# Norm's root put on Y at its eviction, one sum as final update; the second quartic's transposes read without steps; seven sets; the first image without trips

## The chip, the cores and the metric

The kernel runs on one core of a Trainium2 chip. The metric is the device time of one execution in microseconds, the median of several runs. The core has five engines that work through their own instruction lists and wait for each other by semaphores: TensorE (PE, matrix products, with PEld for its weight loads), VectorE (DVE), ScalarE (ACT), GpSimd (POOL) and SyncE (SP), which here only issues transfers. Products land in PSUM, 8 banks of 128x512 floats; DVE and ACT move them from there to SBUF (an eviction).

## The reference

The input is 32 images of 32 channels of 128x128 floats. Two residual layers follow each other; both start with a group norm over pairs of channels (16 groups).

```python
def _L0_conv_ref(A):                       # for each of 1024 matrices
    normA = jnp.sqrt(jnp.sum(A2 * A2, axis=(1, 2)))
    Y = A2 / normA[:, None, None]
    Z = I
    for _ in range(5):
        T = 0.5 * (3.0 * I - jnp.matmul(Z, Y))
        Y = jnp.matmul(Y, T)
        Z = jnp.matmul(T, Z)
    return Y * jnp.sqrt(normA)[:, None, None]
...
x = x + _L0_conv_ref(_gn(x))
x = x + _L1_conv_ref(_gn(x), L1_conv_weights1, L1_conv_weights2)
```

The first layer is five steps of a coupled Newton iteration for a matrix square root, for each of the 1024 matrices. The second is a spectral convolution: a Fourier transform of each image, a 32x32 channel mix on two corners of the spectrum, and the inverse transform.

## The kernel before, in words

**Newton.** The five steps are regrouped into two "quartics" and a last step, so that a matrix needs few products. Four channels form a group, one tile of 128x512; there are 8 groups in an image and 256 in all. `products` makes the four 128x128 products of a group into one PSUM bank, and `transposed` four transposes by TensorE. Each group runs through the generator `newton` (L377), in which every `yield` hands over to the next group. In order it makes: v = plus(mb m) and q = plus(v w) (the first quartic, L347), y from q m, m from q y, mb as the transpose of m, r = mb + eye on GpSimd, then v and q again (the second quartic), then w and y (tile y4) from q m and q y, t = plus(w q), and at last t y, times the root of the norm, added to the input tile xt. `plus` (L269, the sum at L272) evicts on DVE with one scalar_tensor_tensor, `taken` (L261) on ACT.

**Far and near.** The quartic needs w, the transpose of v plus r. For the images below FIRST = 20 ("far") w takes a trip in place of TensorE's time: DVE transposes 32x32 blocks of v into the tile turn (L354), SyncE stores that to a DRAM buffer (L356), loads it back with the blocks in transposed places (L360), and GpSimd adds r (L367). For the other 12 images ("near") TensorE transposes v, and DVE adds r in the eviction. A far group has two trips and 11 sets of four products or transposes, a near group has two sets of transposes more. On the far side the tiles come from the pool `sets` and, in turns, from a second pool `early` (the pair of counts in `rooms`, L249), which is given up when the far groups are done, to make room for the second layer.

**Order.** The main loop (L857) goes round the lanes: LANES = 6 groups are under way at a time, each advances by one `yield` in a round, and a new far group enters every FAR = 17/6 rounds (17 yields in six lanes). Near groups enter every 13/4 rounds, with at most LESS = 4 lanes in use. Beside the lanes, one step of a norm, of the statistics of the next image (`prep`), of the forward transform (`posts`), the spectrum and the inverse (`backs`) is made in a round. The program is recorded in this order; then a planner, which has its own idea of how long instructions take, orders the instructions of each engine. What is wrapped in `kept` keeps its order: the transfers, and the staging. Each engine then works strictly through its list.

**Staging.** `fetch` loads a group twice, as b (from x) and as xt (from the transposed input), and `staged` (L316) applies the norm: b on ACT (L324), and m from xt, two of its four channels on GpSimd (L331) and two on ACT (L324). The four sums at the end of `newton` (L397) multiply by the root of the norm, a value sn for each channel, and add to xt in place. After that `settle` (L405) stores xt, folds it for the forward transform on GpSimd (L412) and takes statistics on DVE (L416).

**Second layer.** When all images of a block of 21, 8 or 3 (GROUPS) have their spectrum, the channel mix (L529, L585) and the inverse transforms (L709 to L783) of that block run between the near groups, or at the end.

The lines that the change touches, and what calls them:

Of the kernel before, what the change touches and what calls it, by code (L numbers as in the profile page):

```python
# [25 lines left out]
ALU = mybir.AluOpType  # L29
# [4 lines left out]
P = 128  # L34
B = 32
C = 32
G = 16
LANES, LESS = 6, 4
FAR, NEAR = 17 / 6, 13 / 4
GROUPS = (21, 8, 3)  # L40


# [5 lines left out]
MS = -QA * QS  # L48
FIRST = GROUPS[0] - 1
# [15 lines left out]
def conv_preact_kernel(  # L65
# [8 lines left out]
    nc = tc.nc  # L74
# [65 lines left out]
    def bank():  # L140
        return ps8.tile([P, 4, P], F32, tag="ps", name="ps")
# [33 lines left out]
    kept = tc.keep_in_program_order  # L175
# [70 lines left out]
        yield  # L246


    rooms = dict(b=(6, 2), xt=(10, 4), x=(4, 2), r=(4, 3), v=(3, 3), w=(3, 3), q=(3, 1), y=(4, 2))  # L249
    rooms.update(m=(3, 2), mb=(2, 1), t=(3, 1), y4=(2, 1), turn=(0, 3))  # L250
    turns = dict.fromkeys(rooms, 0)

    def four(tag, far):
        n, more = rooms[tag]
        if far:
            turns[tag] += 1
            if turns[tag] % (n + more) >= n:
                return early.tile([P, 4, P], F32, tag=tag + "_early", name=tag, bufs=more)
        return sets.tile([P, 4, P], F32, tag=tag, name=tag, bufs=n)

    def taken(ps, tag, far, f=1.0):  # L261
        t = four(tag, far)
        if f == 1.0:
            nc.scalar.copy(t, ps)
        else:
            nc.scalar.mul(t, ps, f)  # L266
        return t

    def plus(ps, f, t, tag, far):  # L269

        s = four(tag, far)
        nc.vector.scalar_tensor_tensor(s, ps, f, t, ALU.mult, ALU.add)  # L272
        return s

    def blocks(t):


        return t.rearrange("p c x -> p (c x)").rearrange("p (a c j) -> p a c j", a=4, c=4)

    def plus_eye(mb, far):  # L280

        r = four("r", far)
        if far:
            nc.gpsimd.tensor_tensor(
                blocks(r).rearrange("p a c j -> p c a j"),
                mb.rearrange("p c (a j) -> p c a j", a=4),
                eye.rearrange("p c (a j) -> p c a j", a=4),
                ALU.add,
            )
        else:  # L290
            nc.gpsimd.tensor_tensor(r, mb, eye, ALU.add)  # L291
        return r

    def products(lhsT, rhs):
        ps = bank()
        for j in range(4):
            nc.tensor.matmul(ps[:, j, :], lhsT[:, j], rhs[:, j], start=True, stop=True)  # L297
        return ps

    def transposed(t):  # L300
        ps = bank()
        for j in range(4):
            nc.tensor.transpose(ps[:, j, :], t[:, j, :], ident)
        return ps

    raw = {}

    def fetch(b, g):
        xt, t = four("xt", b < FIRST), four("b", b < FIRST)
        kept(nc.scalar.dma_start(out=t, in_=x[b, :, 4 * g : 4 * g + 4, :]))  # L310
        kept(nc.scalar.dma_start(out=xt, in_=xt_in[b, :, 4 * g : 4 * g + 4, :]))
        raw[b, g] = xt, t
# [2 lines left out]

    def staged(b, g, nm, sc, offm, sn, scr, off):  # L316

        m = four("x", b < FIRST)
        xt, mb = raw.pop((b, g))

        def on_scalar(t, x, offset, scale, c):
            c = slice(c, c + 1)
            kept(
                nc.scalar.activation(t, x, AF.Identity, bias=offset[:, c], scale=scale[:, c])  # L324
            )

        for j in range(4):
            c = 4 * g + j
            if j < 2:
                kept(  # L330
                    nc.gpsimd.tensor_scalar(  # L331
                        m[:, j, :],
                        xt[:, j, :],
                        nm[:, c // 2 : c // 2 + 1],
                        sc[:, c : c + 1],
                        ALU.add,
                        ALU.mult,
                    )
                )
            else:  # L340
                on_scalar(m[:, j, :], xt[:, j, :], offm, sc, c)
            on_scalar(mb[:, j, :], mb[:, j, :], off, scr, c)
            yield
        ready.append((xt, m, mb, plus_eye(mb, b < FIRST)))
        yield

    def quartic(m, mb, r, far):  # L347


        v = plus(products(mb, m), -1 / (QA * QR * QS), m, "v", far)  # L350
        if far:

            t = four("turn", far)
            nc.vector.transpose(blocks(t), v.rearrange("p c (i b) -> p b c i", b=4))  # L354
            held = dram.tile([P, 512], F32, name="turn", tag="turn", bufs=8)
            kept(nc.sync.dma_start(out=held, in_=t.rearrange("p c x -> p (c x)")))  # L356
            yield
            w = four("w", far)
            kept(
                nc.sync.dma_start(  # L360
                    out=blocks(w).rearrange("p a c j -> p a (c j)"),
                    in_=held.rearrange("(a i) (b x) -> (i b) a x", a=4, b=4),
                )
            )
            yield
            yield
            nc.gpsimd.tensor_tensor(w, w, r, ALU.add)  # L367
            w = blocks(w).rearrange("p a c j -> p c a j")
        else:
            yield  # L370
            w = plus(transposed(v), 1.0, r, "w", far)
        yield
        q = plus(products(v, w), 1 / (16 * QS * QS), eye, "q", far)
        yield
        return q

    def newton(g, sn, xt, m, mb, r, far):  # L377


        q = yield from quartic(m, mb, r, far)  # L380
        y = taken(products(q, m), "y", far, 1 / MS)
        yield
        m = taken(products(q, y), "m", far, MS)
        yield
        mb = taken(transposed(m), "mb", far, QR * QS / MS)
        r = plus_eye(mb, far)
        yield
        q = yield from quartic(m, mb, r, far)
        pw, py = products(q, m), products(q, y)
        w, y = taken(pw, "t", far, 1 / MS), taken(py, "y4", far)  # L390
        yield
        t = plus(products(w, q), -0.5 * EYE / 1.5, eye, "t", far)
        yield
        ps = products(t, y)
        for j in range(4):
            c = 4 * g + j
            nc.vector.scalar_tensor_tensor(  # L397
                xt[:, j, :], ps[:, j, :], sn[:, c : c + 1], xt[:, j, :], ALU.mult, ALU.add
            )
        yield  # L400

    folds = {}
# [389 lines left out]
    def step(queue):  # L792
        if queue and next(queue[0], queue) is queue:
            queue.pop(0)
# [6 lines left out]
    todo = [(b, g) for b in range(B) for g in range(C // 4)]  # L801
    fetches = list(todo)
    stages = list(todo)
    ready = []
# [48 lines left out]
    fetch(*fetches.pop(0))  # L853
    stage()
    fetch(*fetches.pop(0))
    rounds = 0
    while todo or any(lanes) or posts or specs or prods or backs:  # L857
        tail = not todo and not any(lanes)
        if early and len(settled) >= FIRST * (C // 4):
            change()  # L860
        if tail and not posts and not late:

            phase.close()
            late.append(ctx.enter_context(tc.tile_pool(name="late", bufs=1)))
            for kk in range(2, KK):
                late_wts.append(late[0].tile([P, 2, 4, 4, C], F32, name=f"wt{kk}_late"))
                nc.gpsimd.dma_start(out=late_wts[-1], in_=wk[kk])
        for i in range(LANES):
            step(norms)
            far = todo and todo[0][0] < FIRST  # L870
            room = lanes[i] is None and (far or LANES - lanes.count(None) < LESS)
            if todo and room and rounds >= due:
                due = max(due, rounds - 1) + (FAR if far else NEAR)
                while norms:
                    step(norms)
                b, g = todo.pop(0)
                xt = ready[0][0]
                lanes[i] = (b, g, xt, newton(g, made[b][3], *ready.pop(0), far))
                if stages:
                    stage()  # L880
            if lanes[i] is not None:
                b, g, xt, steps = lanes[i]
                if next(steps, lanes) is lanes:
                    lanes[i] = None
                    end(b, g, xt)
            if i == 1:
                step(preps)
            if i == 2 or tail:
                step(specs)
            if i == 3 or tail:  # L890
                step(posts)
            if i == 0 or tail:
                step(prods)
            if i == 0 and (rounds % 5 or len(ended) > B - 6) or tail and not (posts or specs):
                step(backs)
        rounds += 1
# [64 lines left out]
```

## Time and profile before

| | |
|---|---|
| time, median of 3 runs | 3322.49 us (3322.23 to 3326.34) |
| span of the profiled execution | 3310.1 us |
| granted TensorE clock, mean | 0.967 |
| PE, weight loads | 91%, 86% of the span |
| DVE, POOL, ACT | 75%, 58%, 50% |
| POOL sum w (L367), one of 128x512 | 1275 ns, 320 of them |
| ACT eviction, constant factor (L266) | 593 to 598 ns |
| ACT staging of 128x128 (L324) | 482 to 485 ns |
| POOL staging of 128x128 (L331) | 450 ns |

A row of the groups gives the line, engine, operation, tiles written and read with their shape, the count, then busy time and mean length of one, then the idle time of the engine ahead of it with what ended it. Busy time counts overlapping instructions once, so that busy over count is the pace, and the mean is the length of one. A float product of 128x128 is two PE instructions and a transpose is one, so a set of four products is 8 instructions. In the waits a line such as "PE ps <- DVE q" tells how long PE stood still until a DVE instruction that wrote q was done. PE is busiest in every stretch from 100 to 3200 us. The first 100 us are the start, with PE working 55 of them, and the last 110 the tail, where only the last block's inverse is left.

### The profile page before, as it was taken

What the parts mean: (1) busy time and instruction counts of PE and PEld (TensorE: products, weight loads), DVE (VectorE), ACT (ScalarE), POOL (GpSimd) and SP (SyncE); (2) the same over time, 40 slices, a digit from 0 to 9 for tenths busy, and PEclk for the clock granted to TensorE, in tenths of its full rate; (3) what the DMA queues carried; (4) which work ended last, traced back from release to release, by engine and by line L of the source; (5) the groups of instructions that cost most, each with busy time, mean ns of one, the idle gap of its engine ahead of it and who ended that gap; (6) DMA issues with size and microseconds to landing.
All of it is one profiled execution on the core that took longest, in us unless ns stands there. A gap on an engine that the chain in (4) does not pass through costs nothing. (4 is left out here: it accounts for less than half of the span.)

```text
span 3310.1 us, 77971 instructions
## 1 busy us (share of the span) xinstructions
PE 3001.5 (91%) x29376; PEld 2856.1 (86%) x29376; DVE 2477.9 (75%) x6440; ACT 1664.8 (50%) x3588; POOL 1935.0 (58%) x2120
## 2 busy tenths in 40 slices
PE   4999999999999999999999999999899989999854
PEld 4988898998998888899989999888888888898853
DVE  5887888887888887888888676577677767766645
ACT  2555554555555555555555555554455545546533
POOL 3666666666666666667666443255556656635542
PEclk9999999999999999999999999999999999999985
DMA  4656665665666565666665236765656767666577
GB/s 154 210 186 191 185 207 179 198 196 181 197 195 188 185 192 184 198 193 205 188 192 185 94 98 190 226 210 182 211 196 207 251 195 236 208 218 204 182 262 245
DMA packets 485768, 645.85 MB, mean 195 GB/s; under 512 B 91152, under 2 KB 264464, under 8 KB 485392
## 3 DMA queue, kind: packets, MB, share of 16 engines
q1 hardware_dynamic: 369904, 421.66, 39.5%
q10 hardware_dynamic: 113472, 211.86, 20.6%
q0 software_dynamic: 2016, 7.34, 0.6%
q8 instruction: 233, 3.82, 0.5%
q14 instruction: 143, 1.17, 0.1%
HBM read 402.95 MB, written 237.76 MB: 194 GB/s over the span
## 5 line engine op out<-in xcount | busy, mean ns | idle before, releaser
L367 POOL TENSOR_TENSOR w<-w,r 128x512 f32<-128x512 f32 x320 | 407.4, 1275 | 408.7 <-DMA w<-turn 328.9
L297 PE MATMUL ps<-w,v 128*128 128x128 f32 x4096 | 555.5, 279 | 19.3 <-POOL w L367 14.9
L297 PE MATMUL ps<-y,q 128*128 128x128 f32 x4096 | 556.8, 281 | 3.8 <-ACT y L266 3.8
L324 ACT ACTIVATE b<-b,a_off,a_scr 128x128 f32<-128x128 f32 x1024 | 474.0, 485 | 119.8 <-issue 66.6
L297 PEld LDWEIGHTS ps<-w,v 128*128 128x128 f32 x4096 | 505.2, 194 | 28.7 <-POOL w L367 17.2
L297 PEld LDWEIGHTS ps<-y,q 128*128 128x128 f32 x4096 | 513.1, 197 | 6.8 <-ACT y L266 4.9
L412 POOL TENSOR_TENSOR fold<-xt 128x256 f32<-128x256 f32 x512 | 363.8, 730 | 235.0 <-DVE xt L397 209.2
L272 DVE SCALAR_TENSOR_TENSOR q<-ps,eye 128x512 f32<-128x512 f32 x512 | 347.0, 682 | 108.3 <-PE ps L297 106.7
L706 POOL TENSOR_TENSOR yt<-yt,d 128x512 f32<-128x512 f32 x236 | 297.6, 1286 | 161.4 <-ACT d L765 142.2
L297 PE MATMUL ps<-m,q 128*128 128x128 f32 x2048 | 295.2, 289 | 83.3 <-DVE q L272 82.6
L354 DVE STREAM_TRANSPOSE turn<-v 128x512 f32<-128x512 f32 x320 | 357.9, 1119 | 7.0
L297 PEld LDWEIGHTS ps<-m,q 128*128 128x128 f32 x2048 | 259.6, 199 | 101.1 <-DVE q L272 79.0
L291 POOL TENSOR_TENSOR r<-b,eye 128x512 f32<-128x512 f32 x96 | 122.4, 1275 | 346.9 <-issue 294.5
L397 DVE SCALAR_TENSOR_TENSOR xt<-ps,a_t_s,xt 128x128 f32<-128x128 f32 x1024 | 289.6, 340 | 36.9 <-PE ps L297 35.4
L192 DVE BATCH_NORM_STATS2 a_st<-xs 128x6 f32<-128x128 f32 x1024 | 229.2, 278 | 109.1 <-DMA xs<-in_xt 108.8
L266 ACT ACTIVATE t<-ps 128x512 f32<-128x512 f32 x256 | 153.2, 598 | 311.9 <-PE ps L297 288.0
L272 DVE SCALAR_TENSOR_TENSOR v<-ps,x 128x512 f32<-128x512 f32 x256 | 174.9, 683 | 178.9 <-PE ps L297 166.0
L272 DVE SCALAR_TENSOR_TENSOR v<-ps,m 128x512 f32<-128x512 f32 x256 | 175.2, 684 | 174.5 <-PE ps L297 160.1
L297 PE MATMUL ps<-y,t 128*128 128x128 f32 x2048 | 282.7, 282 | 23.5 <-DVE t L272 23.4
L297 PE MATMUL ps<-m,mb 128*128 128x128 f32 x2048 | 279.7, 280 | 18.4 <-ACT mb L266 11.6
L266 ACT ACTIVATE y<-ps 128x512 f32<-128x512 f32 x256 | 152.6, 596 | 276.2 <-PE ps L297 267.4
L297 PE MATMUL ps<-x,b 128*128 128x128 f32 x2048 | 279.1, 280 | 7.3 <-issue 5.6
(124 smaller groups left out, 6052.1 us busy)
## 6 DMA issues: line engine op xcount, KB each, us to landing
turn<-turn SPq DMA_DIRECT2D x320, 256.0 KB
w<-turn SPq DMA_DIRECT2D x320, 256.0 KB
b<-in_x ACTq DMA_DIRECT2D x256, 256.0 KB
xt<-in_xt ACTq DMA_DIRECT2D x256, 256.0 KB
xs<-in_xt ACTq DMA_DIRECT2D x256, 256.0 KB
mid<-xt SPq DMA_DIRECT2D x256, 256.0 KB
yt<-mid SPq DMA_DIRECT2D x128, 512.0 KB
out<-yt SPq DMA_DIRECT2D x108, 512.0 KB
```

The source lines that it names most:

```text
L192: nc.vector.bn_stats(st[:, 4 * i + c, :], tiles[i][:, c, :])
L266: nc.scalar.mul(t, ps, f)
L272: nc.vector.scalar_tensor_tensor(s, ps, f, t, ALU.mult, ALU.add)
L291: nc.gpsimd.tensor_tensor(r, mb, eye, ALU.add)
L297: nc.tensor.matmul(ps[:, j, :], lhsT[:, j], rhs[:, j], start=True, stop=True)
L324: nc.scalar.activation(t, x, AF.Identity, bias=offset[:, c], scale=scale[:, c])
L354: nc.vector.transpose(blocks(t), v.rearrange("p c (i b) -> p b c i", b=4))
L367: nc.gpsimd.tensor_tensor(w, w, r, ALU.add)
L397: nc.vector.scalar_tensor_tensor(xt[:, j, :], ps[:, j, :], sn[:, c : c + 1], xt[:, j, :], ALU.mult, ALU.add)
L412: nc.gpsimd.tensor_tensor(f[:, :, 64 * half : 64 * half + 64], xt[:, :, 0:64], xt[:, :, 64:128], op)
L706: engine.tensor_tensor(yh, yh, d, op)
```

## The change

- **Root on Y.** The factor sn moves from the last sum to the eviction of y4. In place of one copy of 128x512 on ACT there are four scalings of 128x128, each by its channel's sn. The last update becomes one tensor_tensor of 128x512 on DVE in place of four scalar_tensor_tensors of 128x128.
- **Transposes without steps.** In the second quartic of a far group DVE reads v in runs of 32 neighbours instead of every fourth element. The rows that come back must then go elsewhere, which takes four loads of 32 partitions each in place of one of 128. The first quartic stays as it is.
- **Seven sets.** LANES goes from 6 to 7, with buffers added in `rooms`. A far group gets three yields more (one after each q, one after t), so that it lives for 20 rounds, and FAR becomes 20/7.
- **First image without trips.** `is_far` leaves image 0 out, so it goes the near way, with at most four lanes in use. Near images, image 0 among them, now stage all four channels of m on GpSimd.

```diff
-LANES, LESS = 6, 4
-FAR, NEAR = 17 / 6, 13 / 4
+LANES, LESS = 7, 4
+FAR, NEAR = 20 / 7, 13 / 4
...
-    rooms = dict(b=(6, 2), xt=(10, 4), x=(4, 2), r=(4, 3), v=(3, 3), w=(3, 3), q=(3, 1), y=(4, 2))
-    rooms.update(m=(3, 2), mb=(2, 1), t=(3, 1), y4=(2, 1), turn=(0, 3))
+    rooms = dict(b=(6, 2), xt=(10, 5), x=(4, 3), r=(4, 3), v=(3, 3), w=(3, 3), q=(3, 3), y=(4, 3))
+    rooms.update(m=(3, 3), mb=(2, 1), t=(3, 2), y4=(2, 2), turn=(0, 3))
...
+    def is_far(b):
+        return 0 < b < FIRST
...
-            if j < 2:
+            if j < 2 or not is_far(b):
                 kept(
                     nc.gpsimd.tensor_scalar(
...
-    def quartic(m, mb, r, far):
+    def quartic(m, mb, r, far, wide):
...
-            nc.vector.transpose(blocks(t), v.rearrange("p c (i b) -> p b c i", b=4))
+            form = "p c (b i) -> p b c i" if wide else "p c (i b) -> p b c i"
+            nc.vector.transpose(blocks(t), v.rearrange(form, b=4))
...
-            kept(
-                nc.sync.dma_start(
-                    out=blocks(w).rearrange("p a c j -> p a (c j)"),
-                    in_=held.rearrange("(a i) (b x) -> (i b) a x", a=4, b=4),
-                )
-            )
+            wb = blocks(w).rearrange("p a c j -> p a (c j)")
+            if wide:
+                for b in range(4):
+                    rows = slice(32 * b, 32 * b + 32)
+                    src = held[:, P * b : P * b + P].rearrange("(a i) x -> i a x", a=4)
+                    kept(nc.sync.dma_start(out=wb[rows], in_=src))
+            else:
+                src = held.rearrange("(a i) (b x) -> (i b) a x", a=4, b=4)
+                kept(nc.sync.dma_start(out=wb, in_=src))
...
         q = plus(products(v, w), 1 / (16 * QS * QS), eye, "q", far)
         yield
+        if far:
+            yield
         return q
...
-        w, y = taken(pw, "t", far, 1 / MS), taken(py, "y4", far)
-        yield
-        t = plus(products(w, q), -0.5 * EYE / 1.5, eye, "t", far)
-        yield
-        ps = products(t, y)
+        w, y = taken(pw, "t", far, 1 / MS), four("y4", far)
         for j in range(4):
             c = 4 * g + j
-            nc.vector.scalar_tensor_tensor(
-                xt[:, j, :], ps[:, j, :], sn[:, c : c + 1], xt[:, j, :], ALU.mult, ALU.add
-            )
+            nc.scalar.mul(y[:, j, :], py[:, j, :], sn[:, c : c + 1])
+        yield
+        t = plus(products(w, q), -0.5 * EYE / 1.5, eye, "t", far)
+        yield
+        if far:
+            yield
+        nc.vector.tensor_tensor(xt, products(t, y), xt, ALU.add)
         yield
```

More of the change, by code (lines that the diff above doesn't have):

```diff
@@ L304, in transposed @@
         return ps
+    def is_far(b):
+        return 0 < b < FIRST
     raw = {}
     def fetch(b, g):
-        xt, t = four("xt", b < FIRST), four("b", b < FIRST)
+        xt, t = four("xt", is_far(b)), four("b", is_far(b))
         kept(nc.scalar.dma_start(out=t, in_=x[b, :, 4 * g : 4 * g + 4, :]))
@@ L316, in staged @@
     def staged(b, g, nm, sc, offm, sn, scr, off):
-        m = four("x", b < FIRST)
+        m = four("x", is_far(b))
         xt, mb = raw.pop((b, g))
@@ L343, in staged @@
             yield
-        ready.append((xt, m, mb, plus_eye(mb, b < FIRST)))
+        ready.append((xt, m, mb, plus_eye(mb, is_far(b))))
         yield
-    def quartic(m, mb, r, far):
+    def quartic(m, mb, r, far, wide):
         v = plus(products(mb, m), -1 / (QA * QR * QS), m, "v", far)
@@ L374, in quartic @@
         yield
+        if far:
+            yield
         return q
     def newton(g, sn, xt, m, mb, r, far):
-        q = yield from quartic(m, mb, r, far)
+        q = yield from quartic(m, mb, r, far, False)
         y = taken(products(q, m), "y", far, 1 / MS)
@@ L387, in newton @@
         yield
-        q = yield from quartic(m, mb, r, far)
+        q = yield from quartic(m, mb, r, far, True)
         pw, py = products(q, m), products(q, y)
-        w, y = taken(pw, "t", far, 1 / MS), taken(py, "y4", far)
+        w, y = taken(pw, "t", far, 1 / MS), four("y4", far)
+        for j in range(4):
+            c = 4 * g + j
+            nc.scalar.mul(y[:, j, :], py[:, j, :], sn[:, c : c + 1])
         yield
@@ L393, in newton @@
         yield
-        ps = products(t, y)
-        for j in range(4):
-            c = 4 * g + j
-            nc.vector.scalar_tensor_tensor(
-                xt[:, j, :], ps[:, j, :], sn[:, c : c + 1], xt[:, j, :], ALU.mult, ALU.add
-            )
+        if far:
+            yield
+        nc.vector.tensor_tensor(xt, products(t, y), xt, ALU.add)
         yield
@@ L869, in conv_preact_kernel @@
             step(norms)
-            far = todo and todo[0][0] < FIRST
+            far = todo and is_far(todo[0][0])
             room = lanes[i] is None and (far or LANES - lanes.count(None) < LESS)
```

## The prediction

> **What bounds the kernel now.** First the page's busy times, then the same in two stretches (us, then busy us with instruction counts of PE, PE's weight loads, DVE, ACT, POOL; granted clock; DMA): the far images (100 to 1800 us) and the near ones.
>
> ```profile
> PE 3001.5 (91%) x29376; PEld 2856.1 (86%) x29376; DVE 2477.9 (75%) x6440; ACT 1664.8 (50%) x3588; POOL 1935.0 (58%) x2120
> ```
>
> ```profile
> 100.00:1800.00 1700.00, 1600.46 (x13969) 1535.86 (x13969) 1394.08 (x3646) 886.85 (x1900) 1109.18 (x1223) 0.98 0.62 192
> 1800.00:3200.00 1400.00, 1303.55 (x13743) 1231.35 (x13744) 973.67 (x2556) 713.04 (x1550) 759.28 (x825) 0.98 0.60 195
> ```
>
> TensorE is the bound, and no product goes away. What can be won is its idle time: 1700 - 1600 = 100 us in the far stretch, 97 in the near one. DVE is next with 82% of the far stretch. The waits of PE in the far stretch (us in total, times, longest) name the cause:
>
> ```profile
> PE ps L297 <- DVE q L272: 49.4, 42, 3.9
> PE ps L297 <- DVE t L272: 16.6, 24, 3.1
> PE ps L203 <- DVE a_qs L198: 16.1, 11, 3.2
> PE ps L297 <- ACT mb L266: 10.8, 19, 1.4
> PE ps L297 <- POOL w L367: 2.4, 4, 1.8
> ```
>
> Half of it is a product that stands too close behind the DVE sum it reads. One such wait, with what follows it:
>
> ```profile
> 1022.00:1026.00 4.00, 0.34 (x4) 0.15 (x2) 3.97 (x9) 2.56 (x6) 1.54 (x2) 0.81 0.37 131
> 1026.00:1035.00 9.00, 8.97 (x59) 8.24 (x59) 3.69 (x11) 2.66 (x5) 7.14 (x9) 0.70 0.69 177
> ```
>
> DVE works without a break (3.97 of 4.00 us), so q is late because of DVE's backlog. Afterwards PE counts as busy, at a granted clock of 0.70: it starts 59 instructions in 9 us where its full rate of one per 111 ns would start 81. The record of the clock has 13 such dips to 0.5 in the far stretch, of 3.4 us or twice that, 54 us together, so they cost another 27 us. Nearly all begin within 2 to 4 us of the start of a gap of 1.9 us or more, and ten of the thirteen gaps are waits for q (41 of the 54 us).
>
> **What the Trainium skill says.** "TensorE: Matmul & The Clock Gate", Part 1: the array falls to half its clock after an idle window of some 3.4 us. The trace agrees on 0.5 and 3.4 us, though gaps of about 2 us are already enough here. "SBUF — State Buffer", Door 1: accesses stay at full rate with at least two hits per line of 16 bytes. The transposes read every fourth float, one hit per line; no run here shows another step. "ScalarE: Activation LUTs", What ACT_TABLE_LOAD costs: 186 ns + 0.833 ns per element, 93 ns more per pointer operand, 93 ns overlap of neighbours. The trace agrees: L324, two pointers, 128 elements, 485 ns (479 by the page). "DMA: Bandwidth & Descriptors", Why a DMA increments its semaphore by 16: 32 outer rows still spread over 16 engines; no transfer of this trace tells.
>
> The rows that I cost with (count, then busy us and mean ns of one):
>
> ```profile
> L354 DVE STREAM_TRANSPOSE turn<-v 128x512 f32<-128x512 f32 x320 | 357.9, 1119 | 7.0
> L397 DVE SCALAR_TENSOR_TENSOR xt<-ps,a_t_s,xt 128x128 f32<-128x128 f32 x1024 | 289.6, 340 | 36.9 <-PE ps L297 35.4 <-DMA xs<-in_xt 0.2
> L770 DVE TENSOR_TENSOR yt<-ps,yt 128x512 f32<-128x512 f32 x256 | 163.5, 680 | 50.2 <-PE ps L753 43.8 <-DMA yt<-mid 5.4 <-ACT d L765 0.6
> L264 ACT COPY y<-ps 128x512 f32<-128x512 f32 x256 | 149.9, 586 | 72.6 <-PE ps L297 71.4 <-ACT a_r_s L146 0.4 <-issue 0.2
> ```
>
> **Root on Y, one sum.** Four L397 take 4 x 283 = 1.13 us of DVE (busy over count); one sum of PSUM and SBUF is priced like L770, 0.68. DVE gains 0.45 us a group, 115 us in all. On ACT a copy of 0.59 becomes four scalings of 386 ns by the skill (one pointer), with overlaps 1.27: +0.68 us a group. ACT is busy 52% of the far stretch and becomes 58%. Queued behind the scalings are the evictions of y, m and mb.
>
> **Transposes without steps.** Between no gain (1.12 us) and the pace of the other DVE sums of 128x512 (0.68 us); by the page on SBUF the step is what halves the rate, so I take 0.60 to 0.68. That is 0.45 us for each of 152 groups. With the sum, DVE's load falls by 0.9 us in 11 us a group, 82% to about 74%. The price is four reads of 64 KB for one of 256 KB on SyncE. The first trip of the trace shows what matters:
>
> ```profile
> 29.00 1.10 DVE L354 STREAM_TRANSPOSE turn<-v 128x512 f32<-128x512 f32 x1
> 30.13 0.33 SPq L356 DMA_DIRECT2D turn<-turn  x1
> 34.75 0.37 SPq L360 DMA_DIRECT2D w<-turn  x1
> 39.28 1.26 POOL L367 TENSOR_TENSOR w<-w,r 128x512 f32<-128x512 f32 x1 [8.72 <-DMA w<-turn]
> ```
>
> Three more issues of 0.37 us make the last read leave 1.1 us later, and the transpose gives 0.45 back: +0.65 us. The worst I can bound is one more landing in series, 3 us (in the far stretch 2.3 us at the least pass from the issue of a read to the use of w, 3.5 in the median). Following each tile through the far stretch, w is ready 3.7 us (median) before its product, 0.7 us at the 5% point: +0.65 costs few PE waits, +4 us; +3 us would cost about 90 (2 in 5 of 152, by 1.5 us each).
>
> **Seven sets, and a round more after q and t.** This is the large part, and only the built order of instructions shows it. I counted the PE work that stands between the end of a product and the first product that reads its eviction, at 0.89 us a product. For q the far median goes from 2.2 to 5.1 us, and pairs under 2.0 us from 93 of 285 to none; for t (both tiles of that name) from 38 to 20 of 283. For mb it goes the other way: 31 of 143 stand under 1.0 us, 16 under 0.5, where there were none.
>
> What an eviction needs, from the end of its product to its own end, comes from the trace before: q 1.3 us median with a long tail, mb 0.7 and in a quarter of cases over 2.0. Spreading these needs over the distances of the old order gives an estimate of 47 us for q, 20 for t and 6 for mb, against 49.4, 16.6 and 10.8 in the waits: good enough to use. The new order gives q 1.5, t 10, mb 33, m 1.5. DVE's lighter queue takes t to 5 and a_qs from 16 to 11. For mb, in the 16 closest pairs the last product eviction that ACT holds ahead is mostly 4 us old, so little but the 0.75 us eviction itself remains: I take 16, between 11 (no queue) and 68 (the slow tenth every time). Sum: q -48, t -11, a_qs -5, mb +5, m +1, w +4: -54 us.
>
> With q's waits go the ten dips that follow them, 41 us at half speed: -20. The mb waits that come are near 0.75 us each, too short to make new ones.
>
> **First image without trips.** Its first w product starts at 40.6 us after 9.8 us without PE work; a PE transpose and a DVE sum take about 3 us in place of that trip: -10, with later trips of that image under the other sets. 8 groups x 2 transposes x 0.44 us add +7. Staging moves two of four tiles from ACT to POOL in the 104 near groups: -0.8 us ACT, which pays the scalings there, and +0.9 us on POOL, busy 54% there. Net -3; no cost for POOL.
>
> **Near groups.** Their order hardly changes (q pairs under 2.0 us: 40 to 36), DVE gains 0.45 us: 0 to -10. I take 0, since POOL and ACT there get other work.
>
> **Sum.** -54 - 20 - 3 = -77: 3322 - 77 = 3245 us.
>
> **Rivals.** (1) The wait moves to ACT: scalings of 1.27 us ahead of mb, every close pair meets a queue, mb at 68: 52 us more than I take, and its longer gaps keep half of the dips, 10 us: 3307. For it: ACT already makes a quarter of mb's evictions wait; against: 58% load, and the old y evictions ahead. (2) The four reads land one after another, w is late in two of five second quartics: 86 more than I take for w, and the dips stay, 20: 3351, slower. For it: nothing but distance protects it, since the first quartic's trips keep only 9.8 us at the least (11.1 before); against: the transfers carry the same bytes in the same 512-byte pieces. (3) The far stretch gains as I say, but another order in the near part gives it back: within 0.2%, 3320. The near waits show several gaps of 5 us that hang on single backlogs.
>
> **Chances.** Forecast 0.68, rival 1 0.17, rival 2 0.10, rival 3 0.05. Low end: all far waits but a_qs and all dips gone, near -15: 3322 - 80 - 27 - 3 - 15 = 3197, unlikely; I stop at 3208. High end takes in rival 1: 3312. Faster 0.85, same 0.05, slower 0.10.
>
> **What would show it.** Right: in the far stretch PE's wait for q falls under 10 us, PE idles under 60, fewer than 8 dips, the second transposes at 0.6 to 0.7 us, mb on top of the waits. Wrong: w from POOL among the first waits, or mb over 50 us, or the transposes still at 1.12 and DVE over 78%.

## The result and the profile after

The changed kernel takes 3202.2 us (median of 4 runs, 3192.1 to 3218.0) beside 3322.4 us for the kernel before (4 runs, 3313.0 to 3326.3). The ratio is 0.9646 with a 95% interval of 0.9602 to 0.9691: 118 us less by the ratio, where 77 were forecast and 114 was the edge of the range. The profiled execution of before was faster than each of these four (3311.9 us, span 3310) and that of after the slowest of its four (span 3216 us), so the two profiles show 94 us of it. A second profile of the changed kernel, taken with the experiments below, has a span of 3197 us.

The page's busy times of the changed kernel, and its far stretch from 100 us on (columns as in the prediction):

```profile
PE 2973.3 (92%) x29440; PEld 2836.6 (88%) x29440; DVE 2365.3 (74%) x5672; ACT 1716.3 (53%) x4148; POOL 2008.4 (62%) x2312
```

```profile
100.00:1700.00 1600.00, 1529.39 (x13517) 1472.40 (x13516) 1291.47 (x3114) 927.55 (x2288) 1071.78 (x1180) 0.99 0.64 198
```

PE starts 8.45 instructions in a us there, where it started 8.22 before. The waits of PE between 100 and 1800 us of the changed kernel:

```profile
PE ps L298 <- ACT mb L267: 19.6, 21, 3.4
PE ps L298 <- POOL w L376: 14.1, 17, 2.1
PE ps L304 <- ACT m L267: 11.5, 8, 4.2
PE ps L204 <- DVE a_qs L199: 6.3, 6, 2.1
PE ps L298 <- ACT t L267: 3.0, 2, 2.3
PE ps L298 <- DVE q L273: 2.6, 3, 1.5
PE ps L298 <- DVE t L273: 2.4, 1, 2.4
```

The wait for q, 49.4 us before, is 2.6, and mb stands on top. The three operations that the change re-costed, in the rows of the groups (count, busy us, mean ns, idle before):

```profile
L360 DVE STREAM_TRANSPOSE turn<-v 128x512 f32<-128x512 f32 x304 | 277.9, 914 | 7.2
L410 DVE TENSOR_TENSOR xt<-ps,xt 128x512 f32<-128x512 f32 x256 | 173.2, 677 | 46.0 <-PE ps L298 44.3 <-DMA diag<-xs 1.4
L404 ACT ACTIVATE y<-ps,a_t_s 128x128 f32<-128x128 f32 x1024 | 292.1, 369 | 62.3 <-PE ps L298 61.5
```

The mean of 914 ns mixes the two forms of transposes, 1.12 us with steps and about 0.70 us without. The sum takes 0.68 us, and four scalings take 1.14 us (busy over count, times four).

To compare stretches whose ends move, I cut each execution where the last fold of an image ends: the start up to image 1, the far stretch up to image 19, the near stretch up to image 31, and the tail. PE executes almost the same number of instructions in the far and near stretches of both kernels (13202 and 13178; 13223 and 13230).

| us | start | far | near | tail |
|---|---|---|---|---|
| before | 249 | 1608 | 1332 | 122 |
| after | 247 | 1543 | 1306 | 121 |
| after, second profile | 242 | 1540 | 1293 | 122 |

In the far stretch PE's gaps (idle times of 0.15 us or more) go from 94 to 57 us, and the time at half clock from 55 to 31 us, worth 12 us. Shorter interruptions and a few instructions less make up the remaining 17 of the 66 us. In the near stretch, which the prediction left unchanged, gaps go from 84 to 67 us and half clock from 55 to 41, worth 7: together 24 of the 26 us. These are the near stretches of both, before first:

```profile
1857.00:3188.60 1331.60, 1245.39 (x13225) 1177.16 (x13223) 920.19 (x2395) 682.96 (x1482) 719.90 (x778) 0.98 0.61 197
```

```profile
1789.30:3095.10 1305.80, 1237.58 (x13232) 1169.75 (x13231) 884.54 (x2108) 670.99 (x1589) 803.03 (x965) 0.98 0.63 201
```

### The profile page after: what moved, and what is told of

Its sections match the earlier page's. It is cut to its first block, busy times and chain, and to the rows that moved or that the text cites. A ratio compares the mean times of both kernels' runs of the same rounds, so it can differ in the third digit from the quotient of the medians.

```text
span 3216.0 us, 78946 instructions
## 1 busy us (share of the span) xinstructions
PE 2973.3 (92%) x29440; PEld 2836.6 (88%) x29440; DVE 2365.3 (74%) x5672; ACT 1716.3 (53%) x4148; POOL 2008.4 (62%) x2312
## 4 chain that ended last, share of the span: by engine, by line
PE 67%; DVE 13%; DMA 12%; ACT 3%; issue 2%; POOL 1%; SPq 1%; ACTq 0%; DVEq 0%; POOLq 0%
PE ps L298 55%; PE ps L304 6%; DMA xs<-in_xt 5%; DMA turn<-turn 2%; PE ps L764 1%; DMA w<-turn 1%; DVE a_st L193 1%; PE ps L442 1%; DVE turn L360 1%; DVE q L273 1%; DVE yt L781 1%; DVE v L273 1%; PE ps L576 1%; PE ps L742 1%; DVE xt L410 1%
## 5 line engine op out<-in xcount | busy, mean ns | idle before, releaser
L298 PE MATMUL ps<-w,v 128*128 128x128 f32 x4096 | 548.5, 278 | 26.4 <-POOL w L376 14.1
L376 POOL TENSOR_TENSOR w<-w,r 128x512 f32<-128x512 f32 x304 | 386.7, 1275 | 270.5 <-DMA w<-turn 222.0
L328 ACT ACTIVATE b<-b,a_off,a_scr 128x128 f32<-128x128 f32 x1024 | 463.9, 489 | 129.7 <-issue 54.8
L298 PEld LDWEIGHTS ps<-y,q 128*128 128x128 f32 x4096 | 504.7, 194 | 7.0 <-ACT y L267 3.3
L335 POOL TENSOR_SCALAR x<-xt,a_nm,a_sc 128x128 f32<-128x128 f32 x720 | 317.8, 454 | 23.9 <-DVE a_n L222 20.8
L404 ACT ACTIVATE y<-ps,a_t_s 128x128 f32<-128x128 f32 x1024 | 292.1, 369 | 62.3 <-PE ps L298 61.5
L292 POOL TENSOR_TENSOR r<-b,eye 128x512 f32<-128x512 f32 x104 | 132.8, 1277 | 283.8 <-issue 224.6
L298 PE MATMUL ps<-m,q 128*128 128x128 f32 x2048 | 280.3, 280 | 27.9 <-DVE q L273 27.6
L298 PE MATMUL ps<-m,mb 128*128 128x128 f32 x2048 | 282.4, 282 | 19.6 <-ACT mb L267 19.6
L298 PEld LDWEIGHTS ps<-m,q 128*128 128x128 f32 x2048 | 252.1, 194 | 35.4 <-DVE q L273 17.9
L360 DVE STREAM_TRANSPOSE turn<-v 128x512 f32<-128x512 f32 x304 | 277.9, 914 | 7.2
L298 PEld LDWEIGHTS ps<-m,mb 128*128 128x128 f32 x2048 | 254.9, 196 | 27.7 <-ACT mb L267 25.0
```

The costliest lines, as they stand in the source:

```text
L335: nc.gpsimd.tensor_scalar(m[:, j, :], xt[:, j, :], nm[:, c // 2 : c // 2 + 1], sc[:, c : c + 1], ALU.add, ALU.mult,)
L360: nc.vector.transpose(blocks(t), v.rearrange(form, b=4))
L404: nc.scalar.mul(y[:, j, :], py[:, j, :], sn[:, c : c + 1])
```

## The experiments

Two theories were set against each other. *Order*: what counts is the distance, in PE work, between a product and the reader of its eviction, and the list of instructions sets that. *Load*: what counts is DVE's backlog, and the cheaper transposes and sums drained it. Between the versions tested here PE's list is decided by the lanes, the yields and the choice of far images alone. In the traces PE starts the same kinds of instruction in the same order in the kernel before, with the plain transposes alone, with the root alone and with more buffers alone: at most 26 of 29376 places differ, and two executions of the changed kernel differ in 12. The order is also the same in the changed kernel, in each version of it without the root, without the plain transposes or without the near staging, and in the run of its list alone. So the role that the description above gives to a planner doesn't hold for PE between these versions.

### Each part alone

Seven sets alone (the kernel before with these, and the buffers of the change):

```diff
+LANES, LESS = 7, 4
+FAR, NEAR = 20 / 7, 13 / 4
...
         q = plus(products(v, w), 1 / (16 * QS * QS), eye, "q", far)
         yield
+        if far:
+            yield
...
         t = plus(products(w, q), -0.5 * EYE / 1.5, eye, "t", far)
         yield
+        if far:
+            yield
```

> The kernel before with seven sets, their buffers, and the three extra yields of a far group; root, transposes, staging and image 0 as before. Theory order (the distance between a product and the reader of its eviction is what counts): PE's waits for q fall under 10 us between 100 and 1700 us, and this part alone brings 50 to 75 us, the far stretch alone. Rival load (DVE's backlog is what counts, and the lighter DVE of the two other parts drained it): under 30 us, with DVE still above 80% and waits for q or t of 20 us or more left. Neither expects the near stretch to move by more than 10 us.

Measured: 3254.9 us, ratio 0.9775 (0.9742 to 0.9808). PE's waits between 100 and 1700 us:

```profile
PE ps L297 <- POOL w L367: 26.3, 25, 2.6
PE ps L203 <- DVE a_qs L198: 17.8, 11, 4.0
PE ps L297 <- ACT mb L266: 8.8, 3, 6.1
PE ps L303 <- ACT m L266: 6.6, 5, 2.6
```

The wait for q is under 2 us, with DVE as loaded as before (86% of the far stretch, 82% before); this is the order theory's outcome. Far stretch 1561 us (-47), near 1323 (-9). The wait for w, 2.4 us before, has become the first.

Root and one sum alone:

```diff
-        w, y = taken(pw, "t", far, 1 / MS), taken(py, "y4", far)
+        w, y = taken(pw, "t", far, 1 / MS), four("y4", far)
+            nc.scalar.mul(y[:, j, :], py[:, j, :], sn[:, c : c + 1])
...
+        nc.vector.tensor_tensor(xt, products(t, y), xt, ALU.add)
```

> The kernel before with sn on y4's eviction and one sum as last update, six sets and all else as before. Theory order: 0 to -20 us in the far stretch, since q keeps its short distance, with waits for q of 30 us or more. Rival load: -30 us or more, waits for q halved. For the near stretch, which the prediction took as 0 and which came out 26 us shorter: if DVE's lighter sum is the cause, 15 us or more of that is here; if the staging on GpSimd is the cause, under 8.

Measured: 3298.8 us, ratio 0.9915 (0.9893 to 0.9938). PE's far waits:

```profile
PE ps L297 <- DVE q L272: 29.2, 32, 2.8
PE ps L297 <- ACT mb L266: 20.0, 23, 1.5
PE ps L203 <- DVE a_qs L198: 19.3, 11, 3.3
PE ps L297 <- DVE t L272: 15.2, 24, 1.5
```

With an unchanged list the lighter DVE takes q from 49.4 to 29.2 us, and mb goes up from 10.8 to 20.0. The scalings on ACT may have a part in that, but the next run, which has none, also shows 16.1 for mb. Far stretch 1585 us (-23), near 1335 (+3). It lies between the two expectations: load counts where the distance is short.

Plain transposes alone (`quartic` of the changed kernel, all else as before):

```diff
+            form = "p c (b i) -> p b c i" if wide else "p c (i b) -> p b c i"
...
+                for b in range(4):
+                    rows = slice(32 * b, 32 * b + 32)
+                    src = held[:, P * b : P * b + P].rearrange("(a i) x -> i a x", a=4)
+                    kept(nc.sync.dma_start(out=wb[rows], in_=src))
```

> The kernel before with the second quartic's transposes read without steps and four loads for the way back. The second transposes take 0.70 us for 1.12. Theory order: 0 to -15 us, and PE's waits for w from GpSimd rise by 3 to 10 us because the last of four loads leaves 1.1 us later. Rival load: -25 us or more. Nothing in the near stretch.

Measured: 3315.3 us, ratio 0.9974 (0.9958 to 0.9990). Far stretch 1604 us (-4), near 1331. The wait for w stays at 1.8 us, where 3 to 10 more were expected, so the four loads harm nothing while the distance is the old one.

First image and near staging alone:

```diff
+    def is_far(b):
+        return 0 < b < FIRST
...
-            if j < 2:
+            if j < 2 or not is_far(b):
```

> The kernel before with image 0 on the near way and all four channels of near groups staged on GpSimd. The start (up to image 1's last fold) gets 0 to 10 us shorter. Near stretch: if the lighter ACT is the cause of its 26 us, 15 us or more are here; if DVE's one sum is, under 8. Far stretch unchanged within 10 us.

Measured: 3324.7 us, ratio 1.0005 (0.9991 to 1.0018). The start is 250 us with 59 PE instructions more in it, the far stretch 1593 (-15, outside the 10 expected). The near stretch is 1351 us: 19 us longer, which neither theory expected. PE waits 40.2 us in it for the near sum w, where the near waits of before have 3.1 (before first):

```profile
PE ps L297 <- DVE w L272: 3.1, 4, 1.3
```

```profile
PE ps L297 <- DVE w L272: 40.2, 14, 8.0
```

So neither DVE's sum nor ACT's relief, each alone, gives the 26 us that the near stretch gained.

### The changed kernel without one part

Without seven sets (lanes, buffers and yields as before):

> The changed kernel with six sets, the old buffers and no extra yields. PE's list is here the same as in the run of the first image and near staging alone, with 20 of the near pairs of q and 11 of those of w under 2 us apart. Theory order: the far waits for q come back (15 to 35 us, the fewer close pairs of this list) and the near stretch (image 19's last fold to image 31's) is 1325 to 1350 us; time 3270 to 3300. Rival load for the near stretch (lighter ACT and DVE made its 26 us): 1305 to 1315 us.

Measured: 3274.2 us, ratio 0.9868 (0.9830 to 0.9905). Far 1557 us, waits for q 20.8; near 1348 us, as in the run before with the same list. The near waits show what this list does:

```profile
PE ps L298 <- DVE w L273: 29.9, 14, 4.7
PE ps L298 <- DVE q L273: 16.1, 9, 4.2
PE ps L304 <- DVE v L273: 12.2, 10, 3.0
```

Without root and one sum (copy of y4, four sums):

> The changed kernel with the copy of y4 and the four old sums. PE's list is that of the changed kernel, instruction for instruction. Theory order: near stretch stays at 1300 to 1315 us; far stretch 10 to 25 us longer than in the changed kernel, by DVE's load. Rival load: near stretch 1320 us or more. If the four scalings on ACT are what makes m and mb late (far waits 11.5 and 19.6), these fall to about half.

Measured: 3210.6 us, ratio 0.9661 (0.9628 to 0.9693). Far 1541, near 1301 us. The far stretch is no longer than in the changed kernel, where 10 to 25 us more were expected: with this list the heavier sums on DVE cost nothing there. The wait for m falls from 11.5 to 3.8 us, for mb only from 19.6 to 17.8, so the scalings have little part in mb's. They don't make m late by themselves either: below, without the plain transposes but with the scalings, m also has 3.8.

Without the near staging on GpSimd (`if j < 2:` for all):

> The changed kernel with two of four channels of m staged on ACT in near groups too. PE's list unchanged. Theory order: near stretch 1300 to 1315 us, time within 8 us of the changed kernel. Rival (ACT relieved in the near stretch is its gain): 1320 us or more.

Measured: 3198.8 us, ratio 0.9626 (0.9594 to 0.9659). Far 1541, near 1292 us:

```profile
1790.70:3082.40 1291.70, 1234.61 (x13235) 1165.84 (x13233) 879.33 (x2108) 734.32 (x1774) 725.03 (x784) 0.99 0.63 203
```

ACT works 734 us there for 671 in the changed kernel, and the stretch is no longer for it. The near gain is not ACT's relief.

Without plain transposes (steps and one load in both quartics):

> The changed kernel with the second quartic's transposes read in steps as before, one load for the way back. PE's list unchanged. If the four loads are what makes w late (14.1 us), that wait falls under 8 and the time is the same or less; if the faster transpose is worth more than the later load (as the seven sets alone with w at 26.3 us suggest), w rises to 20 to 30 us and the time by 8 to 20 us.

Measured: 3214.5 us, ratio 0.9677 (0.9648 to 0.9706). Far 1538, near 1304, tail 128. The wait for w is 9.0 us for 14.1, and that for a_qs 17.2 for 6.3; the two about cancel in the far stretch. This is neither of the expected outcomes as a whole, since w fell and the time rose. It doesn't show that the four loads make w late either: with the old root and sums w has 18.9 us with four loads (the run without the root) and 24.1 with one (the next run). The 12 us of the medians lie partly in the tail, where no transpose is made, and are hardly clear of the spread.

### The list alone, and what is left in it

Lanes, buffers, yields and first image of the change; root, sums, transposes and staging of before:

> The kernel before with seven sets, their buffers, the extra yields, and image 0 on the near way; the old root and sums, stepped transposes and half the staging on ACT. PE's list is that of the changed kernel, the work of every instruction that of the kernel before. Theory order: the list brings most of the 120 us by itself, near stretch 1290 to 1315 us, time 3215 to 3235. Rival (the other three parts carry it together, each hidden when removed alone): 3250 or more.

Measured: 3217.3 us, ratio 0.9681 (0.9660 to 0.9702). That is 106 of the 118 us by the ratios. Far 1549, near 1297 us. The other three edits together are worth 15 us of the medians on top.

This kernel differs from that of seven sets alone only in the way of image 0, and takes 3217.3 us for 3254.9, 31 us less by the ratios. With six sets the same choice for image 0, with the near staging, brought nothing. Most of it is in the near stretch, far from image 0 (us, in brackets the time of the run):

| near stretch | image 0 far | image 0 near |
|---|---|---|
| six sets | 1332 (3322) | 1351 (3325) |
| seven sets | 1323 (3255) | 1297 (3217) |

So the two edits to the list can't be added up: in these four runs the near gain needs both.

The third extra yield behind mb in place of t (and half of the near staging on ACT):

```diff
         r = plus_eye(mb, far)
         yield
+        if far:
+            yield
...
         t = plus(products(w, q), -0.5 * EYE / 1.5, eye, "t", far)
         yield
-        if far:
-            yield
```

> The changed kernel with the third extra yield moved from behind t to behind mb, and half of the near staging back on ACT. Still 20 yields. In its list no mb stands under 1 us, t stands closer. Theory order: the far wait for mb (19.6) falls under 6 us and that for m falls a little, that for t rises to 5 to 15; time 5 to 20 us less than the changed kernel, 3182 to 3197. Rival (mb is late by ACT's queue, wherever it stands): no gain, waits for mb or m of 15 us or more.

Measured: 3203.1 us, ratio 0.9629 (0.9611 to 0.9648), no better than the changed kernel's 3201.7 in the same batch. Its far waits:

```profile
PE ps L298 <- POOL w L376: 27.4, 23, 3.7
PE ps L298 <- DVE t L273: 23.8, 24, 3.0
PE ps L204 <- DVE a_qs L199: 9.6, 9, 2.6
PE ps L304 <- ACT m L267: 3.6, 4, 2.2
```

The wait for mb is down to 0.6 us, so more distance removes it, with the scalings still on ACT. What was won came back as waits for t and w; I had put t at 5 to 15 us and said nothing of w.

More buffers alone (`rooms` of the change in the kernel before):

> The kernel before with the larger buffer counts alone. Theory order: no change within 6 us, since no wait for a free buffer is seen on PE or DVE. Rival (seven sets gain by their buffers): 15 us or more.

Measured: 3337.3 us, ratio 1.0029 (1.0013 to 1.0045). The buffers bring nothing by themselves and even cost 0.3%, which I can't explain.

The changed kernel again, in the same batch:

> The changed kernel once more, to stand beside the three others on the same chip: 3195 to 3215 us; near stretch 1295 to 1310 us in this profile too if its 26 us are no accident of one execution.

Measured: 3201.7 us, ratio 0.9636 (0.9603 to 0.9669). Far 1540, near 1293 us: the near gain is no accident of one execution.

### What makes the near stretch shorter

The near stretch takes 1284 to 1306 us in every kernel that has PE's near order of the changed kernel (the run with the extra round behind mb has it too), and 1323 to 1351 on three other lists. The question was whether the seventh slot of a round or the phase of the near groups does it. A round also stages once for each slot (`step(norms)`), so the seventh slot changes more than the dealing out.

```diff
+        few = len(todo) < 8 * (B - FIRST) and lanes[6] is None
-        for i in range(LANES):
+        for i in range(6 if few else LANES):
```

> The changed kernel, but once the far groups have left, a round goes over six slots as before. Far list and all instructions as in the changed kernel; only the near stretch is dealt out differently. Theory list (the near stretch's gain is the way its groups and the side work happen to be dealt out): the near stretch (image 19's last fold to image 31's) leaves 1293 to 1306 us for 1315 to 1350, the far stretch stays at 1540 to 1545. Rival work (the near stretch gains by what its instructions cost): 1290 to 1310.

Measured: 3227.3 us, ratio 0.9702 (0.9660 to 0.9745): 25 us of median back, 19 by the ratios, with the far stretch at 1539. The near stretch is 1312 and the tail 128 us.

```diff
+            hold = 9 if todo and todo[0] == (FIRST, 0) else 0
-            if todo and room and rounds >= due:
+            if todo and room and rounds >= due + hold:
```

> The changed kernel, seven slots throughout, with the first near group of image 20 held back for nine rounds after its time; the others follow at the old pace. Theory list: the near stretch moves by 10 us or more either way, beyond the few us of the hold itself. Rival work: 1295 to 1315, the hold included.

Measured: 3206.1 us, ratio 0.9635 (0.9601 to 0.9668); near 1298 us.

> The same with twelve rounds: another phase of the near groups against the side work. Theory list: a near stretch that differs from both the changed kernel's and the nine rounds' by 8 us or more. Rival work: as with nine rounds, within 6 us.

Measured (12 in place of 9): 3215.2 us, ratio 0.9665 (0.9630 to 0.9699); near 1304 us. Two other phases move the near stretch by no more than the profiles of one kernel differ. The number of slots moves the time by more, though its 1312 us fall between what I had put down to the two theories, and are far from the 1331 to 1351 of the lists with six sets throughout. Nor is the seventh slot enough: seven sets alone have it, and 1323 us. So the slot accounts for a part, the way of image 0 for another, and which feature of the near order makes the difference stays open.

One thing that the longest near waits hang on is in the traces of both kernels. PE's longest wait, 7.2 us for v before and 6.4 after, came while DVE itself stood still for the load of an input (xs) whose statistics stand ahead of v in its list (before first):

```profile
2700.63 0.49 DVE L192 BATCH_NORM_STATS2 a_st<-xs 128x6 f32<-128x128 f32 x2 [8.45 <-DMA xs<-in_xt]
```

```profile
2378.17 0.87 DVE L193 BATCH_NORM_STATS2 a_st<-xs 128x6 f32<-128x128 f32 x4 [7.31 <-DMA xs<-in_xt]
```

About 10 us of PE's near gaps fall into such idle time of DVE in either kernel, so this is not what made the stretch shorter.

## Why the prediction was wrong, point by point

- **The bound and its idle time**: right. PE is the bound before and after, and the gain is its idle time and its half clock.
- **Root and one sum**: the sizes were right (DVE 0.68 us, ACT 1.14 for the estimated 1.27 us), and so was that the near groups don't feel it: without it the near stretch is 1301 us.
- **Transposes without steps**: nearly right at 0.70 us (0.60 to 0.68 taken); each of the four issues took 0.43 us in the median, for 0.37 taken. The 4 us for w were put down to the four loads. The wait went up by 12, but seven sets alone, with one load, have 26 us of it, so most of it comes with the list, which the prediction had not charged for w.
- **Seven sets**: the mechanism was right. Of the terms, q came to -47 (-48 forecast), t to -14 (-11), a_qs to -10 (-5), mb to +9 (+5), w to +12 (+4) and m to +11 (+1). m was the one I mis-sized most. It falls to 3.8 us without the scalings and just as far without the plain transposes, so why it is late with both stays open. In gaps the far stretch gave 37 us for the 54 of the sum.
- **Dips**: right in kind; 24 us less at half speed, worth 12, for the 20 forecast. The waits for m, mb, w and the statistics made new ones; the longest for mb was 3.4 us, where the prediction had all near 0.75. With the remainder of 17 us, which the prediction had not counted, the far stretch still came to -66 us for -74. That this is so close is in part luck.
- **First image**: right only for the start, which is 2 us shorter in one profile and 7 in the other, for -3. The term asked what the choice does to image 0 and to the staging, and stopped there. On seven sets it is worth 31 us by the ratios, and in the profiles the near stretch is 26 us shorter for it.
- **Near groups: this is the step that failed.** "Their order hardly changes ... I take 0." The order did change: of the 1484 runs of like PE instructions in the near stretch before, 1298 keep their relative order in the changed kernel, so one in eight moved. With the plain transposes alone none does. The stretch became 26 us shorter, 39 in the second profile, with the list and not with the cost of any instruction: with root, transposes or staging taken back one at a time it stayed at 1292 to 1304 us, and with all three taken back at 1297. Counting pairs of q under 2.0 us (40 to 36) was a poor measure of it; by its recorded expectation the list with image 0 near and six sets has 20 such pairs, and its near stretch is the longest. That the seventh slot also changes a stretch with at most four groups under way had not been considered: taking it away there alone puts 25 us back, to 3227 us, inside the range. What in the new order makes the stretch shorter is not known.
- **Rivals**: the wait for mb on ACT took over the first place but stayed at 20 us of the 68 of rival 1; the trips of rival 2 stayed at 14 us for 90. Neither came near. Rival 3 looked at the right place, the order of the near part, but with the wrong sign.
- **What would show it**: q at 2.6 us, the transposes and mb on top came true. From 100 to 1700 us PE idled 71 us for "under 60" and dipped 8 times for "fewer than 8" (58 us and 6 times between the folds). All these signs lie in the far stretch, so they couldn't tell of the step that failed.

## What to carry to other kernels

When the bound engine works through a fixed list, count how much of its own work stands between a product and the reader of its eviction, and compare with what evictions take, queue included: this told the fate of the largest wait to within 2 us before any run, and the list alone later gave nine tenths of the gain. But a list is shared: the choice for the first image made a stretch 1500 us later 26 us shorter with seven sets and, with the near staging, 19 us longer with six. So try edits to the list together as well as singly, and time every stretch that they reach: a count of close pairs that hardly moved didn't mean that the time would not. When each wait sits at the edge of its distance, moving slack from one to another can gain nothing, as from t to mb here.

## What the runs showed of the hardware

- A 32x32-block transpose of 128x512 floats on DVE takes 1.12 us when it reads every fourth float, 0.70 when it reads neighbours. The Trainium skill ("SBUF — State Buffer", Door 1) has lines of 16 bytes with at least two hits needed for full rate. This agrees in direction; the page gives no size for it.
- PE goes to half clock after single gaps of about 2 us in these traces (1.9 us at 1561 us of before, 2.1 us at 287 us of after), though not after each, and stays there for 3.4 us or a multiple. The Trainium skill ("TensorE: Matmul & The Clock Gate", Part 1) has an idle window of about 3.4 us; the length of the dips agrees with it, and the gaps that were enough are shorter.
- Scalings of 128x128 from PSUM with one pointer take 369 ns each, 285 ns busy in sequence; an estimate by the prices of the Trainium skill ("ScalarE: Activation LUTs", What ACT_TABLE_LOAD costs) is 386 and 293.
